# A planner that keeps TensorE's rows divided, and layer-0 aggregations noted one behind the other

## The chip, the cores and the metric

The kernel runs on one core of a Trainium2 chip. The metric is the device time of one execution in microseconds (us). The kernel before takes 3310.98 us, the median of three runs (3309.94 to 3311.04).

## What is computed

x holds 128 graphs of 64 nodes with 512 features each, all float32; adj is one 64 x 64 matrix of zeros and ones that all graphs share. Four layers follow one another, each as `x = layernorm(x + layer(x, adj))`:

```python
# layer 0: messages weighted by adj
out = deg * (x @ Wi.T + b) + adj @ (x @ Wj.T)
# layer 1: attention with 4 heads, attention with one, then two dense layers and a layernorm
h   = elu(softmax(mask(leaky(f1_i + f2_j))) @ (x @ W_heads))      # 4 heads, side by side
o   = elu(softmax(mask(leaky(g1_i + g2_j))) @ (h @ W_out))
y   = relu(o @ w1 + b1) @ w2 + b2 + o                             # then layernorm, gamma, beta
# layers 2 and 3: attention with one head
out = softmax(mask(leaky(e_src_i + e_dst_j))) @ (x @ W)
```

## The kernel before, in words

**Tiles.** Two graphs of 64 nodes fill the 128 partitions of one tile; two tiles make a pair (T = 2), and there are 32 pairs, p = 0 to 31. A pair goes through all four layers before it leaves the chip. Many pairs are under way at once, about one new one every 100 us.

**Products.** Most dense products are done in Strassen's way: `seven` (L633) makes seven products of halves where eight would be needed. It keeps two PSUM tiles, named stx and sty in the profile (sty holds two quarters of the result, y and z). Products 0, 2 and 4 go into sty, products 1, 3, 5 and 6 into stx, and each time VectorE (DVE) adds the result to its place in SBUF before the next product may start in the same tile. stx_h and sty_h are the heads of layer 1, stx_o and sty_o the projection by W_out, stx_y and sty_y the product by w2; stx_0, stx_2 and stx_3 are layers 0, 2 and 3 (the profile leaves the numbers out). The weights for these products are prepared once: `stage_stream` (L580) loads the four quarters of a matrix (raw_wo, raw_w, raw_W), lets GpSimd (POOL) form their differences T1 to T4, and stores all seven to a buffer in HBM (d_wo, d_w, d_W); `part_from` (L613) loads a part from there for each product (ws_wo, ws_w, ws_W). The raw quarters and the parts of the larger matrices share one ring of four SBUF buffers.

**Aggregations.** Where adj (or an attention matrix) is applied to x, a graph has only 64 nodes, so a matmul would use only 64 rows of TensorE. The kernel divides the rows: two matmuls, one per graph, stand in the upper and the lower 64 rows. This is so in `stage_first` (L887, layer 0: axp from x and aggr), in `stage_scores` (L937, layer 1's heads: yp from x and aT) and in `stage_out` and `stage_tile` (op from who and aT, 64 rows by 64 columns). Everything else uses all 128 rows. Layer 0's aggregation of one tile is eight matmuls into two PSUM tiles; ScalarE (ACT) copies them to the buffer ax, of which there is one. The first four pairs (p < AHEAD = 4) then multiply by W0 directly (l0); the later ones go through `strassen` with the stored parts of W0.

**Attention.** Scores come from dot products on DVE (or, for pairs 0 and 1, from a small matmul fp on transposed x, x1Tp); bc is their broadcast on TensorE, e the softmax on DVE and ACT, pt the transposed result, aT (aTg in layers 2 and 3) its copy by ACT, gp the aggregation in layers 2 and 3, oTp a transpose before w1, hidp the product by w1.

**What sets the order.** No instruction is issued where it is written. Every stage is a generator; the stages are run by a queue with due times (L1300 to L1330), and each call on an engine is only noted as a Step (`note`, L188). Calls inside `nc.together()` make one Step. A Step's rank is its place in the order of noting, less SOON = 1000 inside `nc.soon()`, plus corrections from the table LATER (L48), by engine and name and, with /S and /E, for the first 11% and the last 7% of the Steps only. Then `order` (L229) plays through all Steps with a simple cost of each (`cost`, L353): whenever an engine is free, it gets the ready Step of lowest rank. PSUM and SBUF buffers are handed out in this play as well: a Step that opens a tile waits for a free buffer, in the order of noting, and NEAR (L42) says how far a later Step may go ahead of an earlier one. SLACK (L43) is time allowed for a result to reach another engine. The order found is then issued, and each engine runs its own part in that order. SyncE (SP) issues all DMAs, so its order is that of the loads and stores.

Of the kernel before, what the change touches and what calls it, by code (L numbers as in the profile page):

```python
# [38 lines left out]


WAIT = 0.152
NEAR = 150  # L42
SLACK = {"tensor": 0.8, "sync": 0.4}  # L43

LATER = {  # L48
    "gp:never/S": -100, "gp:rs_i": -60, "gp:s_o/S": -20, "gp:ys/E": -40, "sc:aT": -100,
    "sc:aTg/S": 20, "sc:elu/S": -40, "sc:hT": 120, "sc:oT": 60, "sc:who": -80, "sc:xT": -200,  # L50
    "sc:xT/S": -180, "sc:ys/S": 132, "sy:beta/S": -12, "sy:raw_w": 180, "te:fp/S": -20,
    "te:hidp/E": -40, "te:hidp/S": 28, "te:l": 29, "te:l/S": 69, "te:pt": -28, "te:pt/E": 200,
    "ve:e": -29, "ve:e/S": 40, "ve:f_o/S": -120, "ve:hT": 100, "ve:has": 200, "ve:mv": -100,
    "ve:mv/E": 100, "ve:mx": -20, "ve:o": -140, "ve:r": -40, "ve:r/E": 40, "ve:sh": 10,
    "ve:sm": -80, "ve:st": -13,
}


# [105 lines left out]
class Plan:  # L164
# [23 lines left out]
    def note(self, engine, name, args, kw):  # L188
        if self.joined:
            s = self.joined[0]  # L190
            assert s.engine == engine
        else:
            s = Step(engine, len(self.steps) - self.early)
            self.steps.append(s)
            if self.joined is not None:
                self.joined.append(s)
        out = [kw[k] for k in ("out", "accum_out") if k in kw] + (
            [] if "out" in kw or not args else [args[0]]
        )
        views = [(v, True) for v in out if isinstance(v, View)] + [  # L200
            (v, False)
            for v in [*args, *kw.values()]
            if isinstance(v, View) and not any(v is o for o in out)
        ]
        for v, writes in views:
            t = v.tile
            writes = writes or t.pool.space is PSUM
            if not t.seen:
                s.opens.append(t)
            else:  # L210
                s.behind.add(t.seen[0][0])
            s.uses.add(t)
            s.after.update(o for o, r, w in t.seen if (w or writes) and v.meets(r))
            t.seen.append((s, v.region, writes))
        s.after.discard(s)
        s.behind -= {s} | s.after
        s.calls.append((name, args, kw))
        if not s.kind:
            what = out[0].tile.args.get("name", "?") if out and isinstance(out[0], View) else "dram"
            what = re.sub("__+", "_", re.sub(r"\d+", "", what).rstrip("_"))  # L220
            s.kind = f"{engine[:2]}:{what}"
        takes, s.lands = cost(engine, name, args, kw, out)
        if engine in ("vector", "gpsimd"):

            both = [v for v, writes in views if not writes and v.tile.pool.space is not PSUM]
            s.port = len(both) > 1 and (engine == "vector" or size_of(out) > 2)
        s.takes += takes

    def order(self):  # L229
# [2 lines left out]
        free = dict.fromkeys(engines, 0.0)  # L232
        coming = {e: [] for e in engines}
        there = {e: [] for e in engines}
        wire, port, out = 0.0, 0.0, []
        then = {s: [] for s in self.steps}
        for i, s in enumerate(self.steps):
            s.no, s.ready, s.waits = i, 0.0, len(s.after) + len(s.behind)
# [54 lines left out]
        while len(out) < len(self.steps):  # L293
            at, e = min(
                (free[e] if there[e] else max(free[e], coming[e][0][0]), e)
                for e in engines
                if there[e] or coming[e]
            )
            while coming[e] and coming[e][0][0] <= at:
                s = heapq.heappop(coming[e])[3]  # L300
                heapq.heappush(there[e], (s.rank, s.no, s))
            s = heapq.heappop(there[e])[2]
            if s.port and port > at:
                at = port
# [48 lines left out]
def cost(engine, name, args, kw, out):  # L353

    size = size_of(out)
    if engine == "tensor":
        if name == "transpose":
            return size * 0.00085, 0.0

        beside = P * P // math.prod(kw["lhsT"].shape)  # L360
        return (
            size * 0.00169 if beside == 1 else 0.208 / beside + 0.0003 * size
        ), 0.0
    if engine == "sync":
        return 0.06, 0.0015 * size
    if name == "tensor_tensor_reduce":
# [7 lines left out]
def gnn_stack_kernel(  # L374
# [512 lines left out]
    def stage_first(p):  # L887
# [3 lines left out]
            yield 0.3 * TURN  # L891

        ax = unit.tile([P, 2, T, KC, P], FP, tag="ax", name=f"ax_{p}")
        for t in range(T):
            x = xs[p][:, t, :]
            ps = [
                psum.tile([P, KC, 2, N], FP, tag="b", name=f"axp_{p}_{t}_{b}")
                for b in range(2)
            ]
            with nc.together():  # L900
                for c in range(KC):
                    for b in range(2):
                        nc.tensor.matmul(
                            ps[b][:, c, :, :], lhsT=x[ts(b, N), ts(c, P)],
                            rhs=aggr[ts(b, N), 0 if p < AHEAD else t, :, :], start=True, stop=True,
                        )
            with nc.soon():
                for b in range(2):
                    nc.scalar.copy(
                        ax[:, :, t, :, ts(b, N)], ps[b].rearrange("p c s i -> p s c i")  # L910
                    )
            nc.gpsimd.tensor_tensor(x, x, degb, ALU.add)
            yield 3.0
            if p < AHEAD:
                ps = psum.tile([P, D], FP, tag="b", name=f"l0_{p}_{t}")
                for k in range(KC):
                    with nc.together():
                        for s in range(2):
                            nc.tensor.matmul(
                                ps, lhsT=ax[:, s, t, k, :], rhs=w0[s][:, k, :],  # L920
                                start=(k == 0 and s == 0), stop=(k == KC - 1 and s == 1),
                            )
                    if k == 1:
                        yield 4.0
                nc.vector.tensor_tensor(x, ps, x, ALU.add)
                normalize(x, f"0_{p}_{t}")
                yield 4.0
        if p >= AHEAD:
# [464 lines left out]
```

## Time and profile before

| | |
|---|---|
| median of three runs | 3310.98 us |
| the profiled execution | 3313.95 us |
| its span, first to last instruction | 3312.2 us |
| mean granted TensorE clock | 0.994 |
| TensorE busy | 3265.2 us (99%), 21268 passes |
| VectorE (DVE) busy | 2374.4 us (72%) |
| GpSimd (POOL) busy | 1724.0 us (52%) |
| ScalarE (ACT) busy | 1364.6 us (41%) |
| DMA queue, share of 16 engines | 67.1%, 722 MB |

PE is TensorE's matmul, PEld its weight load. A line of the timeline gives the start, the length, the engine, the line of the code (nearly all have L336, as one helper issues everything), what is written from what, the rows and columns in use (64*128 is a divided matmul), and how many instructions are merged. A float32 matmul appears as two passes, a transpose as one. A line of waits gives the waiting engine and tile, whom it waited for, and the total, the number and the longest. A line of the table by stage gives the stretch, its width, the busy time of each engine with its number of instructions, the mean granted TensorE clock, the share of DMA and GB/s.

### The profile page before, as it was taken

To read this page: it belongs to the slowest core of one execution; us is meant where nothing else is said; L and a number is where in the kernel's file an instruction comes from. 1 tells how busy PE (TensorE), PEld (TensorE's weight loads), DVE (VectorE), ACT (ScalarE), POOL (GpSimd) and SP (SyncE) were. 2 spreads that over 40 slices of the span, in tenths; PEclk is the share of its full clock that TensorE was granted. 3 is DMA by queue.
4 is the path that set the end of the run, shared out by engine and by line. 5 is a ranking of instruction groups with operands and counts; after the bars stand their busy time and mean duration, and the time that the engine had idled before them with its cause. 6 is when DMAs were issued, how large, how long until landed. Compare 5 with 4: busy or idle time off the path is not lost.

```text
span 3312.2 us, 60000 instructions
## 1 busy us (share of the span) xinstructions
PE 3265.2 (99%) x21268; PEld 2881.8 (87%) x21268; DVE 2374.4 (72%) x5668; ACT 1364.6 (41%) x3226; POOL 1724.0 (52%) x1860
## 2 busy tenths in 40 slices
PE   8999999999999999999999999999999999999997
PEld 4888888898988989989889988888889899898885
DVE  5467767777777777777777777777777767777766
ACT  2434344343444434444443443434444344343442
POOL 6745445554555555455454555645554455554442
PEclk9999999999999999999999999999999999999998
DMA  8956666767667676667766667676666766667652
GB/s 303 338 177 215 221 203 215 234 208 237 211 210 233 213 247 197 200 230 221 242 204 220 212 217 236 214 226 208 214 233 208 246 201 202 229 216 238 227 183 77
DMA packets 306584, 726.08 MB, mean 219 GB/s; under 512 B 34240, under 2 KB 43504, under 8 KB 306288
## 3 DMA queue, kind: packets, MB, share of 16 engines
q1 hardware_dynamic: 306288, 722.26, 67.1%
q8 instruction: 171, 2.80, 0.3%
q14 instruction: 125, 1.02, 0.1%
HBM read 688.69 MB, written 33.44 MB: 218 GB/s over the span
## 4 chain that ended last, share of the span: by engine, by line
PE 91%; DVE 4%; DMA 3%; POOL 1%; issue 1%; ACT 0%; SPq 0%; POOLq 0%; DVEq 0%; ACTq 0%
PE stx_h L336 13%; PE stx_o L336 13%; PE stx L336 12%; PE sty_h L336 10%; PE sty_o L336 9%; PE sty L336 9%; PE hidp L336 7%; PE yp L336 4%; PE gp L336 3%; PE stx_y L336 3%; PE sty_y L336 2%; PE axp L336 2%; PE l L336 1%; PE op L336 1%; PE oTp L336 1%; DMA d_f<-f 1%
## 5 line engine op out<-in xcount | busy, mean ns | idle before, releaser
L336 DVE CUSTOM_DVE_ANT_0 j<-x,rows 128x512 bf16<-128x512 f32 x736 | 584.1, 794 | 94.3 <-DMA rows<-d_h 75.6
L336 PE MATMUL stx_h<-ys,wh 128*128 128x128 f32 x3072 | 403.8, 275 | 0.7 <-DVE hT L336 0.7
L336 PEld LDWEIGHTS stx_h<-ys,wh 128*128 128x128 f32 x3072 | 381.1, 192 | 22.3 <-DVE sh L336 5.7
L336 POOL TENSOR_SCALAR rs<-mv 128x1 f32<-128x1 f32 x256 | 104.1, 407 | 406.2 <-DVE mv L336 392.2
L336 ACT COPY hT<-stx_h 128x256 f32<-128x256 f32 x384 | 143.0, 372 | 384.6 <-PE stx_h L336 378.6
L336 ACT ACTIVATE x<-x,sh,rs 128x512 f32<-128x512 f32 x256 | 207.2, 813 | 223.6 <-DVE sh L336 221.0
L336 PE MATMUL sty_h<-ys,wh 128*128 128x128 f32 x2048 | 273.8, 277 | 0.0
L336 PEld LDWEIGHTS sty_h<-ys,wh 128*128 128x128 f32 x2048 | 254.4, 192 | 9.0 <-issue 0.5
L336 PE MATMUL stx_o<-ws_wo_T,s_o 128*128 128x256 f32 x1024 | 246.0, 383 | 0.5 <-ACT who L336 0.5
L336 DVE TENSOR_TENSOR x<-stx,x 128x256 f32<-128x256 f32 x360 | 150.8, 420 | 132.1 <-PE stx L336 131.0
L336 PE MATMUL sty_o<-ws_wo,hT 128*128 128x256 f32 x1024 | 243.2, 380 | 0.1
L336 PE MATMUL hidp<-oT,w 128*128 128x256 f32 (+1 forms) x1056 | 228.9, 373 | 0.0
L336 PEld LDWEIGHTS hidp<-oT,w 128*128 128x128 f32 x1056 | 194.0, 190 | 24.9 <-ACT oT L336 0.2
L336 PEld LDWEIGHTS stx_o<-ws_wo_T,s_o 128*128 128x128 f32 x1024 | 190.2, 191 | 28.4 <-ACT who L336 2.1
L336 PEld LDWEIGHTS sty_o<-ws_wo,hT 128*128 128x128 f32 x1024 | 190.8, 191 | 25.6 <-issue 1.1
L336 DVE SCALAR_TENSOR_TENSOR hT<-elu,hT 128x512 f32<-128x512 f32 x256 | 174.9, 684 | 43.3 <-ACT elu L336 41.3
L336 POOL TENSOR_TENSOR ys<-ys,t 128x256 f32<-128x256 f32 x128 | 102.9, 814 | 189.8 <-PE sty_h L336 189.4
L336 ACT ACTIVATE elu<-hT 128x512 f32<-128x512 f32 x256 | 153.0, 599 | 108.7 <-DVE hT L336 104.6
L336 POOL TENSOR_TENSOR rs<-rs,mhalf 128x1 f32<-128x1 f32 x256 | 173.4, 677 | 21.1
L336 DVE BATCH_NORM_STATS2 st<-x 128x6 f32<-128x512 f32 x256 | 176.5, 689 | 5.1
L336 DVE TENSOR_TENSOR hT<-sty_h,hT 128x256 f32<-128x256 f32 x256 | 107.2, 420 | 81.2 <-PE sty_h L336 69.3
L336 ACT COPY ys<-yp 128x512 f32<-128x512 f32 x256 | 132.2, 602 | 78.4 <-PE yp L336 71.7
(205 smaller groups left out, 7629.3 us busy)
## 6 DMA issues: line engine op xcount, KB each, us to landing
ws_wo_T<-d_wo_T SPq DMA_DIRECT2D x256, 512.0 KB, 3.9
ws_wo<-d_wo SPq DMA_DIRECT2D x192, 512.0 KB, 5.3
ws_W_T<-d_W_T SPq DMA_DIRECT2D x248, 256.0 KB, 4.2
rows<-d_h SPq DMA_DIRECT2D x240, 256.0 KB, 4.7
ws_w_T<-d_w_T SPq DMA_DIRECT2D x112, 512.0 KB, 4.9
ws_W<-d_W SPq DMA_DIRECT2D x186, 256.0 KB, 4.1
ws_w<-d_w SPq DMA_DIRECT2D x84, 512.0 KB, 5.2
rows<-d SPq DMA_DIRECT2D x128, 256.0 KB, 4.3
```

Of the source, the lines that this page charges most:

```text
L336: getattr(getattr(self.tc.nc, s.engine), name)(*map(real, args), **{k: real(v) for k, v in kw.items()})
```

## The change

Four things change together:

1. `note` marks a matmul whose stationary operand is smaller than 128 x 128 as tiled. When the planner chooses TensorE's next Step and the last one was tiled, it takes a ready tiled Step ahead of all others.
2. The planner's costs: a change between tiled and other Steps takes 0.2 us; a tiled matmul is priced by half its columns.
3. In `stage_first`, for pairs from 4 on, the aggregations of both tiles are noted directly one behind the other, ahead of ACT's copies; before, tile 1's came after tile 0's copies and an addition on POOL. For the first four pairs the order of noting is as before.
4. NEAR goes from 150 to 176, SLACK for sync from 0.4 to 0.403, and the table LATER has other entries, so that ranks move on every engine.

```diff
-NEAR = 150
-SLACK = {"tensor": 0.8, "sync": 0.4}
+NEAR = 176
+SLACK = {"tensor": 0.8, "sync": 0.403}
...
-    "gp:never/S": -100, "gp:rs_i": -60, "gp:s_o/S": -20, "gp:ys/E": -40, "sc:aT": -100,
...
+    "gp:ax": -120, "gp:raw_w/S": 60, "gp:raw_wo/S": -60, "gp:rs_i": -40, "gp:rs_i/E": -60,
+    "gp:t": -160, "gp:t/E": 100, "gp:ys": 20, "sc:elu": -112, "sc:f/S": -80, "sc:who/S": -120,
+    "sc:x": 40, "sc:ys": -160, "sc:ys/S": 120, "sy:b_sb/S": -80, "sy:beta/S": -3,
+    "sy:d_w_T": -260, "sy:d_wo_T": 100, "sy:degb": -120, "sy:w": 40, "sy:wh": 7, "te:bc_o": -80,
+    "te:fp": -60, "te:gp/E": 11, "te:hidp/S": 28, "te:l/S": 131, "te:pt/E": 200,
+    "te:stx/S": -20, "te:stx_h/E": 27, "te:stx_y/S": -28, "te:sty_o/E": -240, "te:xTp": -120,
...
+        s.tiled = "lhsT" in kw and math.prod(kw["lhsT"].shape) < P * P
...
-            s = heapq.heappop(there[e])[2]
+            s = None
+            if rows and e == "tensor":
+
+                more = [c for c in there[e] if c[2].tiled]
+                if more:
+                    s = min(more)
+                    there[e].remove(s)
+                    heapq.heapify(there[e])
+                    s = s[2]
+            s = s or heapq.heappop(there[e])[2]
+            if e == "tensor":
+                at += 0.2 * (s.tiled != rows)
+                rows = s.tiled
...
-        return (
-            size * 0.00169 if beside == 1 else 0.208 / beside + 0.0003 * size
-        ), 0.0
+        return size * 0.00169 / beside + 0.005 * (beside > 1), 0.0
...
         ax = unit.tile([P, 2, T, KC, P], FP, tag="ax", name=f"ax_{p}")
+        ps = {}
+
+        def turn(t):
+            for b in range(2):
+                ps[t, b] = psum.tile([P, KC, 2, N], FP, tag="b", name=f"axp_{p}_{t}_{b}")
+            for c in range(KC):
+                for b in range(2):
+                    nc.tensor.matmul(
+                        ps[t, b][:, c, :, :], lhsT=xs[p][ts(b, N), t, ts(c, P)],
+                        rhs=aggr[ts(b, N), 0 if p < AHEAD else t, :, :], start=True, stop=True,
+                    )
+
+        if p >= AHEAD:
+            for t in range(T):
+                with nc.together():
+                    turn(t)
         for t in range(T):
             x = xs[p][:, t, :]
-            ps = [
-                psum.tile([P, KC, 2, N], FP, tag="b", name=f"axp_{p}_{t}_{b}")
-                for b in range(2)
-            ]
-            with nc.together():
-                for c in range(KC):
-                    for b in range(2):
-                        nc.tensor.matmul(
-                            ps[b][:, c, :, :], lhsT=x[ts(b, N), ts(c, P)],
-                            rhs=aggr[ts(b, N), 0 if p < AHEAD else t, :, :], start=True, stop=True,
-                        )
+            if p < AHEAD:
+                with nc.together():
+                    turn(t)
```

More of the change, by code (lines that the diff above doesn't have):

```diff
@@ L41 @@
 WAIT = 0.152
-NEAR = 150
-SLACK = {"tensor": 0.8, "sync": 0.4}
+NEAR = 176
+SLACK = {"tensor": 0.8, "sync": 0.403}
 LATER = {
-    "gp:never/S": -100, "gp:rs_i": -60, "gp:s_o/S": -20, "gp:ys/E": -40, "sc:aT": -100,
[L50 to L55, printed above, removed]
+    "gp:ax": -120, "gp:raw_w/S": 60, "gp:raw_wo/S": -60, "gp:rs_i": -40, "gp:rs_i/E": -60,
[4 more added lines that the diff above has]
+    "te:stx/S": -20, "te:stx_h/E": 27, "te:stx_y/S": -28, "te:sty_o/E": -240, "te:xTp": -120,
+    "ve:abd": -120, "ve:e": -29, "ve:e/S": 40, "ve:e_o/E": 140, "ve:f_o/E": 160,
+    "ve:f_o/S": -120, "ve:gT": 340, "ve:mv": -100, "ve:mv/E": 140, "ve:mv_i/E": -80,
+    "ve:o": -100, "ve:r": -60, "ve:sh": 49, "ve:sm": -60, "ve:st": -20, "ve:st_i": -20,
+    "ve:st_i/S": -40, "ve:who": -140,
 }
@@ L234, in order @@
         there = {e: [] for e in engines}
-        wire, port, out = 0.0, 0.0, []
+        wire, port, rows, out = 0.0, 0.0, False, []
         then = {s: [] for s in self.steps}
@@ L909, in stage_first @@
                     nc.scalar.copy(
-                        ax[:, :, t, :, ts(b, N)], ps[b].rearrange("p c s i -> p s c i")
+                        ax[:, :, t, :, ts(b, N)], ps[t, b].rearrange("p c s i -> p s c i")
                     )
@@ L914, in stage_first @@
             if p < AHEAD:
-                ps = psum.tile([P, D], FP, tag="b", name=f"l0_{p}_{t}")
+                l0 = psum.tile([P, D], FP, tag="b", name=f"l0_{p}_{t}")
                 for k in range(KC):
@@ L919, in stage_first @@
                             nc.tensor.matmul(
-                                ps, lhsT=ax[:, s, t, k, :], rhs=w0[s][:, k, :],
+                                l0, lhsT=ax[:, s, t, k, :], rhs=w0[s][:, k, :],
                                 start=(k == 0 and s == 0), stop=(k == KC - 1 and s == 1),
@@ L924, in stage_first @@
                         yield 4.0
-                nc.vector.tensor_tensor(x, ps, x, ALU.add)
+                nc.vector.tensor_tensor(x, l0, x, ALU.add)
                 normalize(x, f"0_{p}_{t}")
```

## The prediction, made before the changed kernel ran

> **What bounds the kernel now.** First the busy times, for the whole span and by stage; then TensorE's waits; then its timeline at the places that these name; last, the instruction orders of both kernels. Page, part 1:
>
> ```profile
> span 3312.2 us, 60000 instructions
> PE 3265.2 (99%) x21268; PEld 2881.8 (87%) x21268; DVE 2374.4 (72%) x5668; ACT 1364.6 (41%) x3226; POOL 1724.0 (52%) x1860
> ```
>
> TensorE is the bound. By stage (width, then busy time by engine):
>
> ```profile
> 0.00:300.00 300.00, 281.89 (x1710) 224.09 (x1711) 179.12 (x423) 112.61 (x257) 178.86 (x169) 0.98 0.76 259
> 300.00:3200.00 2900.00, 2894.01 (x19159) 2591.96 (x19158) 2123.51 (x5044) 1216.36 (x2874) 1512.11 (x1635) 1.00 0.68 220
> 3200.00:3313.00 113.00, 89.27 (x403) 65.73 (x401) 71.75 (x203) 35.62 (x96) 33.08 (x57) 0.89 0.29 92
> ```
>
> In the loop TensorE is idle 6 of 2900 us; the head and the tail have 18 and 24. So a gain can come only from fewer TensorE microseconds of work, or from head and tail. A matmul here is two passes. A pass's price is start to start over its count (TensorE's timeline: start, length, group):
>
> ```profile
> 1502.92 1.03 PE L336 MATMUL sty<-ws_W_T,gT 128*128 128x256 f32 x4
> 1503.78 1.05 PE L336 MATMUL stx_h<-ys,wh 128*128 128x128 f32 x8
> 1504.67 1.03 PE L336 MATMUL stx<-ws_W_T,s 128*128 128x256 f32 x4
> ```
>
> ```profile
> 1029.12 1.89 PE L336 MATMUL stx_o<-ws_wo_T,hT 128*128 128x256 f32 x8
> 1030.95 2.95 PE L336 MATMUL yp<-aT,x 64*128 64x128 f32 x48
> 1033.83 1.99 PE L336 MATMUL stx<-ws_w_T,s 128*128 128x256 f32 x8
> 1035.75 0.49 PE L336 MATMUL yp<-aT,x 64*128 64x128 f32 x4
> ```
>
> Four 256-column passes take 0.86 us (0.215 each), eight 128-column passes 0.89 (0.111). Divided passes go two at a time: 24 pairs should take 24 x 0.111 = 2.67 us. Now the switches: before the divided stretch 8 x 0.215 = 1.72, but 1.83 are used (+0.11); the stretch uses 2.88 (+0.21); the eight passes after it 1.92 (+0.20, of which about half belongs to the next stretch). **One stretch of divided rows costs 0.40 us** for going in and out, whatever its length. Priced so, TensorE's starts leave 28 us lost at 0 to 300, 11 in the loop, 28 after 3200 (half-speed passes counted too). TensorE's waits in the head (total, times, longest), then in the tail:
>
> ```profile
> PE stx_o L336 <- DVE who L336: 2.5, 1, 2.5
> PE x1Tp L336 <- ACT ax L336: 2.0, 1, 2.0
> PE pt_1o L336 <- DVE e_1o L336: 1.6, 1, 1.6
> PE sty_h L336 <- POOL t L336: 1.5, 1, 1.5
> PE stx_o L336 <- DMA ws_wo<-d_wo: 1.1, 1, 1.1
> ```
>
> ```profile
> PE bc L336 <- DVE f L336: 6.0, 3, 3.5
> PE sty L336 <- ACT gT L336: 2.4, 1, 2.4
> ```
>
> **What the Trainium skill says.** "TensorEngine Tiling (Array Packing)", Key Properties: a change of tiling mode drains TensorE. The trace agrees: 0.40 us per stretch. "TensorE: Matmul & The Clock Gate", Part 1: the clock has two rates, full and half, decided in windows of about 3.4 us. The trace agrees: the 2 us wait of x1Tp at 66 us is followed by layer-0 passes of 0.85 us in place of 0.43, and the window 70 to 74 us has a mean clock of 0.72. So a wait of 2 us can cost a further 1 to 2. "DMA: Bandwidth & Descriptors", Queues, rings and completion order: each DMA engine takes descriptors in ring order. At the start the landings do follow SP's order, about 0.65 us per 256 KB.
>
> **Part 1, the switches.** Both orders hold the same matmuls (10,996 calls), so only stretches count. Before: 165 (71 of yp, 62 of axp, 32 of op). After: 158 (65, 55, 32, and 6 of axp with yp). The rule does little: the two axp groups of a pair stand next to each other in one of the 28 later pairs; in the others a PSUM buffer comes free 2.1 to 5.1 us of TensorE work later, and something else goes in between. 7 x 0.40 = **-2.8 us**, all on the bound. Lower price 0.2 (only the drain in): -1.4; higher 0.5: -3.5.
>
> **Part 2, the start.** The new table reorders SP's queue: degb (256 KB) and b1 go ahead of adj; x_1, x_2, x_3 ahead of w0; rows_a and wh between w0's chunks. adj landed at 2.7 and 3.4 us and TensorE began at 4.7; behind degb I put it 2 us later (nearest row: degb took 1.7 us in its place; range 1 to 4). In return pair 1's aggregation, which had to await x_1 until 15.3 us, now fills early time, while w0's last chunk (some 6.5 MB down the queue, which the trace of before had moved by 21.5 us) comes at about 22 us and is wanted at about 25. To the first axp of pair 2 I count 28.2 us after, 28.4 before: **0**, range -1 to +4. DVE now has six wh dot products ahead of the first x_0 addition; their weights land by about 21.6, the addition is due at 26: no cost.
>
> **Part 3, x1Tp.** It stood behind ax's copies, which wait for the one ax buffer, which waits for l0_2_1. Its wait and the slow passes after it cost 2.15 + 0.39 + 1.35 = 3.9. In the new order x1Tp of pair 1 goes 13 us of work earlier; what now follows l0_2_1 is bc (0.86), half of fp (0.9), then l0_3_0, which needs two ax copies (2 x 0.59 and some 0.5 on the way, 1.7): covered, up to 0.3 left. **-3.8**, range -3.9 to -2.
>
> **Part 4, the first projection.** At 126 to 134 us TensorE loses 1.67 + 0.35 + 1.23 = 3.3 to POOL's t1 and the load of ws_wo. POOL does t1 two long operations earlier in the new order, so the first wait goes (-3.3). But TensorE then comes some 5 us earlier to a chain that does not move with it: the four ws buffers pass from raw_wo1 to raw_w0 to ws_wo, released by POOL's raw_w0 operations (2.36 us each) and by stores and loads of 4 to 5 us. Raw_w0's third operation ends at about 122 us in place of 124.4, as t1 and t2 (2 x 1.27) now stand ahead of it; the first ws_wo lands 5 us later, at 127; TensorE is there at 122.5. New wait **+4.2**, range 0 to +7. Behind it on TensorE's queue everything waits.
>
> **Part 5, 195 to 290 us.** The last product of pair 1's projection waited for DVE's addition to who with 0.4 us of work in between; now 2.2. With yp behind it, 2.70 + 0.57 + 1.13 = 4.4 were lost; I leave 0.9: **-3.5**, range -4.4 to -1. gp of pair 0 after pt: 0.53 + 1.05 lost, cover 1.1 and 2.6 us in place of 0.9 and 0.9: **-1.3**. oTp of pair 0 has lost one 1.7 us group of its cover: **+0.5**, range 0 to 1.5. The wait at pt_1o of pair 0 (2.7 of work between bc_1o and pt_1o in both) stays.
>
> **Loop and tail: 0.** Loop links keep their cover: pt to gp 2.6 us or more in both, op to oTp 4.7 and 4.8, pt to yp 3.6 in place of 1.9. Thinner are axp to the first product of layer 0 (3.2 us in six pairs, never under 5.8; it needs about 1.7) and pt_1o to op (2.9 for 3.6). The tail has the same sequence from hidp of pair 31 on, and two of its largest waits stand at the same places (bc of pair 30, gT of pair 30). Range -2 to +4 for both together.
>
> **Sum.** -2.8 + 0 - 3.8 - 3.3 + 4.2 - 3.5 - 1.3 + 0.5 = **-10.0**. The profiled execution took 3313.95 (span 3312.2 and 1.8 around it), so 3304.0 in its terms; the median of the runs is 3.0 below it, 3310.98, so **3301.0**.
>
> **Rivals.** (a) The head's waits only move: POOL, stores and loads are as late as before, and parts 3 to 5 give nothing. For it: POOL is busy 179 of the first 300 us, and part 4 is such a case. Against it: x1Tp and who had their causes in the order alone. Left: part 1, 3308.2. (b) The chain of part 4 moves along with TensorE (POOL's earlier operations start earlier, as they hang on DVE's dot products): no new wait, -14.2, 3296.8. (c) Slower: two aggregations noted behind one another hold four of the eight PSUM buffers until ACT has copied them, and the first product of layer 0 follows in six of the 28 pairs after 3.2 us. If that starves TensorE by more than 10.0/28 = 0.36 us in each of 28 pairs, the gain is gone; at 0.85 (24 us in all) it ends at 3325. Against it: in the loop ACT waits for axp (215 us in all) and TensorE never waits for ax there. (d) The change doesn't do what it says: taken into part 1, as 165 to 158 shows.
>
> **Chances.** The forecast 0.43; (b) 0.19; (a), with a late start or half of parts 3 and 5 missing, 0.28; (c) 0.10. A difference of 0.2% (6.6 us) is about what a measurement here can tell from no change: faster means under 3304.4, slower over 3317.6. The forecast and (b) are faster, 0.62; (a) is the same, 0.28; (c) slower, 0.10. Range: from part 1 to 5's better ends, 3293, to (a) with the start 3 us late, 3311; outside lie (c) and a little at either end.
>
> **What would show it.** Part 1: divided stretches 158 in TensorE's timeline, each still 0.40. Part 2: TensorE's first matmul at 6 to 7 us, pair 2's axp at 28. Part 3: no wait of x1Tp. Part 4: a wait of sty_o or stx_o for ws_wo of about 4 us near 122 to 128. Part 5: who's wait under 1 us. Loop: idle time as before, under 10 us. I am wrong if the loop shows a wait that repeats with every pair, or if the head's loss stays near 28 us.

## The result: slower by 6 us, and the profile after

| | before | after |
|---|---|---|
| median, 18 runs each | 3310.28 us | 3316.74 us |
| ratio, 95% interval | | 1.0017 (1.0011 to 1.0024) |
| span of the profiled execution | 3312.2 us | 3317.1 us |

The forecast was 3301.0, its range 3293 to 3311: wrong in sign. Page of the changed kernel, part 1:

```profile
span 3317.1 us, 59898 instructions
PE 3263.4 (98%) x21268; PEld 2880.5 (87%) x21268; DVE 2363.1 (71%) x5668; ACT 1364.7 (41%) x3226; POOL 1697.4 (51%) x1860
```

TensorE's passes are as many as before. By stage (width, then busy time by engine, the last three columns the mean TensorE clock, the DMA engines' busy share and GB/s):

```profile
0.00:300.00 300.00, 281.65 (x1720) 225.82 (x1721) 184.50 (x425) 113.87 (x258) 176.45 (x170) 0.98 0.77 261
300.00:3200.00 2900.00, 2887.63 (x19117) 2586.18 (x19116) 2103.52 (x5028) 1213.97 (x2871) 1483.84 (x1630) 1.00 0.68 219
```

In the loop TensorE is idle 12.4 us where it was idle 6.0. The prediction's own measure, the time between TensorE's starts beyond the prices of passes and switches ("the loss" from here on), sorts the 4.9 us between the two spans (the last column is a second profile of the changed kernel):

| loss, us | before | after | after again |
|---|---|---|---|
| ahead of the first matmul | 4.7 | 5.2 | 5.8 |
| 0 to 100 | 11.0 | 8.2 | 7.6 |
| 100 to 200 | 11.0 | 17.1 | 13.2 |
| 200 to 300 | 6.5 | 0.5 | 0.8 |
| loop, 300 to 3200 | 11.1 | 22.3 | 23.1 |
| tail | 27.4 | 26.1 | 26.8 |

The switches give back their 2.8 us, the stretch from the first matmul to 300 us 2.7 (in the second profile 6.9) and the tail 1.3; the first matmul comes 0.5 later, and the loop takes 11.2. TensorE's waits in the loop, before and then after (total, times, longest):

```profile
PE pt L336 <- DVE e L336: 1.9, 2, 1.1
PE sty_y L336 <- DMA ws_w<-d_w: 1.3, 2, 0.9
PE stx_o L336 <- DMA ws_wo_T<-d_wo_T: 1.1, 2, 0.6
```

```profile
PE sty_y L352 <- DMA ws_w<-d_w: 3.2, 7, 0.8
PE stx_o L352 <- DMA ws_wo_T<-d_wo_T: 2.5, 6, 0.9
PE pt L352 <- DVE e L352: 1.6, 2, 1.0
PE sty_y L352 <- DMA ws_w_T<-d_w_T: 1.2, 2, 0.7
```

In the changed kernel no wait is longer than 1 us, but there are many, and the new ones are above all for DMAs, for the parts of w2 that sty_y and stx_y multiply by. Counted as loss, the products of w2 went from 2.9 us to 10.9. These parts come through the second ring of the kernel (six buffers of 256 KB for the parts of w2, W2 and W3): a load can leave only when a buffer comes free, a median of 6.5 us ahead of its use and in a quarter of the cases under 5.2, and then has to land. In the kernel before it is the same: 6.6, and a quarter under 5.2. So the change did not take time from these loads. The page's DMA view (count, size, median us from issue to landing) of before, then of after:

```profile
ws_w_T<-d_w_T SPq DMA_DIRECT2D x124, 256.0 KB, 3.6
ws_w<-d_w SPq DMA_DIRECT2D x93, 256.0 KB, 2.9
```

```profile
ws_w_T<-d_w_T SPq DMA_DIRECT2D x124, 256.0 KB, 4.2
ws_w<-d_w SPq DMA_DIRECT2D x93, 256.0 KB, 3.9
```

These medians rest on 37 and 45 of w2's 217 loads, those whose landing the page tells. Worked out from the semaphore updates in the trace for 215 of the 217, the mean went from 4.1 to 4.5 us and the median from 4.0 to 4.3; the slowest quarter begins at 5.2 us in place of 4.6. So the same transfers take some 0.4 us longer in the new order, and most of it lies in the slow ones.

### The profile page after: what moved, and what is told of

It reads as the page before. It is cut to its first block, busy times and chain, and to the rows that moved or that the text cites. A ratio compares the mean times of both kernels' runs of the same rounds, so it can differ in the third digit from the quotient of the medians.

```text
span 3317.1 us, 59898 instructions
## 1 busy us (share of the span) xinstructions
PE 3263.4 (98%) x21268; PEld 2880.5 (87%) x21268; DVE 2363.1 (71%) x5668; ACT 1364.7 (41%) x3226; POOL 1697.4 (51%) x1860
## 4 chain that ended last, share of the span: by engine, by line
PE 88%; DMA 6%; DVE 3%; POOL 2%; issue 1%; SPq 0%; ACT 0%; POOLq 0%; DVEq 0%; ACTq 0%
PE stx_h L352 13%; PE stx_o L352 12%; PE stx L352 11%; PE sty_h L352 10%; PE sty_o L352 9%; PE sty L352 8%; PE hidp L352 7%; PE yp L352 3%; PE gp L352 3%; PE stx_y L352 2%; PE l L352 2%; DMA over<-d_f 2%; PE axp L352 1%; PE sty_y L352 1%; DMA ws_wo_T<-d_wo_T 1%; DMA d_f<-f 1%
## 5 line engine op out<-in xcount | busy, mean ns | idle before, releaser
L352 POOL TENSOR_SCALAR rs<-mv 128x1 f32<-128x1 f32 x256 | 88.7, 347 | 387.8 <-DVE mv L352 334.5
L352 POOL TENSOR_TENSOR s<-gT 128x256 f32<-128x256 f32 x62 | 48.1, 776 | 225.3 <-DVE gT L352 169.0
L352 DVE SCALAR_TENSOR_TENSOR sh<-mv,rs 128x1 f32<-128x1 f32 x256 | 105.3, 412 | 79.9 <-POOL rs L352 79.5
```

What stands on the lines that cost most here:

```text
L352: getattr(getattr(self.tc.nc, s.engine), name)(*map(real, args), **{k: real(v) for k, v in kw.items()})
```

## The experiments

Labels with a_ are edits of the changed kernel, with b_ of the kernel before. Each ran beside the kernel before on the same chip; "ratio" is to it. The kernel before took between 3308.0 and 3312.3 us beside them, so experiments are compared by their ratios, not by their times. With half-widths of about 0.0008, two ratios are told apart from some 0.001 (3.5 us) on.

**Is it the ring, the start, or what is in the way?** a_wk7 and b_wk7: `bufs` of the ring 6 to 7 in the real tiles only, so no order changes. To make room, layer 0's bias rows are added where beta's belong, which leaves beta out of the result (that edit isn't shown).

```diff
+MORE = {'wk': 7}
...
-            self.made = self.pool.real.tile(self.shape, self.dtype, **self.args)
+            args = dict(self.args)
+            if args["tag"] in MORE:
+                args["bufs"] = MORE[args["tag"]]
+            self.made = self.pool.real.tile(self.shape, self.dtype, **args)
```

> The changed kernel, every engine's order as it is, but with 7 buffers in place of 6 in the ring that holds the parts of w2, W2 and W3 (to make room, POOL adds layer 0's bias rows where beta's rows belong; beta is still loaded, into a tile that nothing reads). My theory: of the 11.2 us that the loop lost against the kernel before, 8.0 stand ahead of products of w2, whose parts are loaded only when a buffer of this ring comes free, 4 to 7 us before their use, and land 4 to 5 us later. A seventh buffer lets each load start one part earlier (about 0.9 us or more), so the losses at w2's products fall from 10.9 us to 1 to 3 us and the kernel is 7 to 10 us faster than the changed one: 3307 to 3310, ratio to the kernel before 0.999 to 1.000. Rival, late starts elsewhere: the losses at w2's products only mark where TensorE meets a delay of DVE or POOL that stands behind it; then they move to another product and the time stays within 2 us of 3316.7. Rival, two aggregations holding four of eight PSUM buffers: no effect, 3316 to 3317.

> The kernel before with the same seventh buffer and the same substitution of bias rows. My theory: its products of w2 lose only 2.9 us in the loop, so it gains 1 to 3 us: 3307 to 3309, ratio 0.9990 to 0.9997, and the two kernels then stand within 2 us of each other where they stood 6.4 apart. Rival, delays of other engines: no gain here either, and the difference of 6 us stays.

a_wk7: 3313.27 us, 1.0007 (0.9999 to 1.0015): against the changed kernel's 1.0017 and 1.0022 a gain of 3 to 5 us, at the edge of what can be told apart and about half of what I had expected. Loads left 0.6 to 0.7 us earlier, but w2's mean landing time rose from 4.5 to 4.9 us; the loss at w2's products fell only to 9.2. b_wk7: 3311.03, 1.0000 (0.9992 to 1.0009), no gain; there too the landing time rose, from 4.1 to 4.4. In both, about half of the head start was lost again on the way.

a_start puts three loads back in front, a_rows moves two broadcasts behind a part of w2, both on SP's queue alone (a_start's edit is shown):

```diff
-            for s in self.order():
+            out = self.order()
+            first = [s for s in out if s.kind in ("sy:adj_i", "sy:x")][:3]
+            for s in first + [s for s in out if s not in first]:
```

> The changed kernel with one edit: on SP's queue the two loads of adj and the first of x_0 go ahead of degb and b1 again, all else as in the changed kernel. The prediction put the late start at 0 up to pair 2's first aggregation. My theory now: TensorE's first matmul comes 1 to 2 us earlier and part of that reaches the first projection at 96 us, where TensorE then waits for ws_wo all the same; so it gains 0 to 2 us, 3315 to 3317. Rival: the start is the larger part of the missing gain in the head, and the kernel is 3 us or more faster.

> The changed kernel with one edit: in the 13 pairs whose score rows of layer 2 (two broadcasts of 256 KB) are issued between w2's parts 21 and 22, SP issues them behind part 22; every other engine's order is the same. My theory: what makes w2's loads late is the company that they land in; without these two transfers ahead of them T2 and 22 land about 1 us or more earlier in these 13 pairs, whose losses at w2's products (3.4 us in sum) go, and the kernel is 2 to 4 us faster, 3313 to 3315. Rival, the ring alone sets the landing (loads start as late as before): less than 1 us.

a_start: 3317.81, 1.0020 (1.0014 to 1.0027), nothing gained: the first matmul came at 4.1 us but the first aggregation at 8.0 (7.0), and pair 2's at 28.5 (27.9). a_rows: 3319.44, 1.0028 (1.0017 to 1.0039), nothing gained either. In its profile w2's products lost 7.5 us in place of 10.9, as expected, but the loop still lost 23.1: pt lost 5.1 (2.8), sty_o 5.0 (1.7). The loss had moved.

**Which part of the change?** v1_oldtable keeps rule and costs and takes the old table, NEAR and SLACK; v4_norule takes the rule out (`s = heapq.heappop(there[e])[2]`, no 0.2); v6_lat3 plans landings 1 us later (`s.end = wire + 3.0`).

> The changed kernel (rule for divided rows, price of a switch and of divided matmuls, both tiles' aggregations noted together) with the table, NEAR and SLACK of the kernel before. The order that it gives has 149 divided stretches (158 in the changed kernel, 165 before), 16 x 0.40 = 6.4 us less of switches than before. My theory: it is the new table that sets w2's loads among other transfers, not the rule; then the loop loses 11 to 15 us (22.3 in the changed kernel), of which 3 to 5 at w2's products, and the kernel runs in 3304 to 3310. Rival, the rule: taking divided groups out of their rank makes every just-in-time load tighter; then the loop loses 18 us or more here too, and the time is 3312 or more.

> The changed kernel with its new table, costs and noting, but without the rule in the planner: TensorE's next group is again the first by rank, and no switch is priced. 160 divided stretches, 0.8 us more of switches than the changed kernel. My theory (the table): the loop loses 18 us or more, 3314 to 3320. Rival (the rule): the loop loses about 11 us as before the change, and with the head's gains of 2.7 us the time is 3305 to 3310.

> The changed kernel with one number changed in the planner: a load is planned to land 3.0 us after its transfer in place of 2.0 (parts of w2 take 4.5 us from issue to landing in the trace of the changed kernel, 2.8 in the old plan). 147 divided stretches, 4.4 us less of switches. My theory: the loop's losses are loads that land later than planned, so with 1 us more planned the losses at w2's products fall from 10.9 to 2 to 5 us, and the kernel runs in 3303 to 3309, faster than the changed one by 8 to 13 us. Rival: TensorE then meets the next tight thing (the attention chain before pt, POOL's sums before the projection's products), as in the run with the score rows moved; then the loop loses 17 us or more and the gain is that of the switches alone, 3310 to 3313.

> The changed kernel once more, as a reference beside the others, and for a second profile of it: how far do the losses of one execution repeat? My theory: the loop loses 20 to 26 us again, 9 to 13 of it at w2's products, and the time is 3315 to 3318. Rival: the losses at w2's products are those of one execution; then they fall under 5 us here.

v1_oldtable 3370.34 (1.0180, 1.0166 to 1.0194), v4_norule 3345.49 (1.0108, 1.0093 to 1.0123), v6_lat3 3370.55 (1.0180, 1.0166 to 1.0194), after_again 3318.13 (1.0022, 1.0013 to 1.0030). The first three loop losses are 68, 36 and 68 us, spread over almost every product.

All three expectations were too low by 25 to 60 us; of the rivals only v1_oldtable's, which was open upward (3312 or more), holds the result. Rule and table can't be judged apart: in these runs each half without its own other half costs far more than the 6 us in question, so splitting them says nothing of either. One part can be split off: with the rule, costs and table of the changed kernel, noting both tiles' aggregations behind one another (point 3 of the change) makes no difference at all. The planner's order is the same on all five engines without it. The second profile confirms the loop's loss (23.1, of which 13.1 at w2's products).

**Taking TensorE's waits away, all transfers made, orders unchanged.** a_free and b_free let w2's products read resident columns; a_wo does so for pair 0's first projection. (The condition on `dims` leaves the loads themselves as they are.)

```diff
+                if v.tile.args.get("name", "").startswith("ws_w2") and v.dims != [0, 1, 2]:
+                    v = self.w1[:, v.region[1][0], 0:256]
+                return v.real()
```

> The changed kernel with every load and every engine's order as they are, but the products of w2 read columns of w1, which are resident, in place of the parts of w2 that are loaded for them; so TensorE no longer waits for these loads (the second matrix of the feed-forward layer is left out of the result; the transfers are all still made). Known by now: the loop of the changed kernel loses 22.3 and 23.1 us in two profiles, 10.9 and 13.1 of it at w2's products; moving other transfers out of the way of w2's loads lowered that to 7.5 but pt and the projection's products lost 6 us more. My theory: the late loads of w2 are the loss that the change added; without them the loop loses 11 to 14 us and the kernel runs 8 to 12 us faster than the changed one, 3305 to 3309, ratio to the kernel before 0.998 to 0.9995. Rival: the order is tight everywhere, and TensorE, being earlier, meets the attention chain and POOL's sums instead; then the loop loses 18 us or more and at most 4 us are gained, 3312 or more.

> The kernel before with the same edit: w2's products read resident columns of w1, all loads and orders stay. Theory: its loop loses 2 to 3 us at w2's products, so it gains 1 to 4 us, 3307 to 3310, and stands within 2 us of the changed kernel with the same edit, or behind it. Rival: no gain, 3310 to 3313, and the changed kernel with the edit stays 3 us or more behind it.

> The changed kernel, all loads and orders as they are, but the seven products of pair 0's first projection read columns of w1 in place of the loaded parts of W_out (that piece of the projection is left out of the result for this pair). It prices the new wait of part 4: in two profiles TensorE waited 4.2 and 4.1 us at its first product for the load, and passes at half speed and a second wait followed, 9 to 10 us less 2 in sum. Theory: the loss from 100 to 200 us falls from 13 to 17 us to 5 to 8, and the kernel is 6 to 9 us faster, 3308 to 3311. Rival: POOL's sums or the who additions stand right behind the load, and 3 us or less are gained.

a_free: 3318.63, 1.0024 (1.0015 to 1.0033). b_free: 3312.31, 1.0002 (0.9994 to 1.0011). My theory fell: TensorE no longer waited for w2, and nothing was gained. Loop and waits of a_free:

```profile
300.00:3200.00 2900.00, 2886.20 (x19111) 2586.41 (x19110) 2103.46 (x5030) 1213.57 (x2870) 1482.27 (x1630) 1.00 0.68 219
```

```profile
PE pt L357 <- DVE e L357: 5.9, 6, 1.3
PE sty L357 <- DMA ws_w<-d_w: 2.6, 4, 1.1
PE stx L357 <- DVE x L357: 1.6, 3, 0.6
```

TensorE is as idle as in the changed kernel (13.8 us; 12.4 there), and the loop loses 22.0 us: pt 7.3 where it was 2.8.

The edit had a side effect, though. Where no product reads a buffer, the next load into it waits for the landing of the one before, and SP's queue is held at other places. SP's own waits in the loop, in the changed kernel and in a_free:

```profile
SPq L352 <- DMA ws_w<-d_w: 1.1, 3, 0.5
SPq L352 <- DMA ws_w_T<-d_w_T: 2.5, 6, 0.7
```

```profile
SPq L357 <- DMA ws_w<-d_w: 50.5, 38, 3.8
SPq L357 <- DMA ws_w_T<-d_w_T: 12.2, 19, 1.7
```

In return, SP's waits for stx_y and sty_y fell from 84 us to 10. So part of what a_free lost elsewhere may be of its own making, and that it gained nothing doesn't prove that w2's waits cost nothing.

a_wo: 3318.29, 1.0022 (1.0014 to 1.0030), no gain; the wait for ws_wo, 4.0 us at the first group of the projection, came as 5.7 us at the next group of the same projection, and 100 to 200 us lost 14.3 (17.1 and 13.2 in the changed kernel).

**A second chain beside the first.** The pt that wait over 1 us in a_free are those of pairs 8, 16, 18, 24 and 26, in the heads' attention. Its way is f2p (TensorE), a store d_f, two loads over, DVE's e, pt. In pairs 8, 10, 16, 18, 24 and 26 the change cut TensorE's work between f2p and pt from 26.8 us to 23.4. The first part of the way has grown as well. Pair 16 before (TensorE's, SP's and DVE's timelines):

```profile
1606.25 0.27 PE L336 MATMUL f2p<-ident,f 128*8 128x128 f32 x1
...
1633.15 0.60 PE L336 MATMUL pt<-ident,e 128*128 128x128 f32 x4
```

```profile
1605.85 0.92 SPq L336 DMA_DIRECT2D ws_w_T<-d_w_T  x2
1606.86 0.29 SPq L336 DMA_DIRECT2D d_f<-f  x1
...
1611.76 1.12 SPq L336 DMA_DIRECT2D over<-d_f  x2
```

```profile
1630.90 0.69 DVE L336 TENSOR_TENSOR e<-bc,r 128x512 f32<-128x512 f32 x1
```

and after:

```profile
1607.62 0.27 PE L352 MATMUL f2p<-ident,f 128*8 128x128 f32 x1
...
1631.37 0.63 PE L352 MATMUL pt<-ident,e 128*128 128x128 f32 x4
```

```profile
1608.79 1.18 SPq L352 DMA_DIRECT2D ws_w_T<-d_w_T  x2
1610.07 0.29 SPq L352 DMA_DIRECT2D d_f<-f  x1
...
1615.27 1.10 SPq L352 DMA_DIRECT2D over<-d_f  x2
```

```profile
1630.53 0.69 DVE L352 TENSOR_TENSOR e<-bc,r 128x512 f32<-128x512 f32 x1
```

Before, d_f leaves 0.6 us after f2p's start; after, 2.4, since it stands on SP's queue behind parts T3 and T4 of w2, which wait for their buffers; over leaves 7.6 us after f2p in place of 5.5. e is done at 1631.22, pt starts 0.15 later, so it was waited for; before, e was done 1.56 us ahead of pt. (From f2p to e's end it is 23.6 us; before it was 25.3, with nothing that hurried it.) So two chains run beside each other, w2's loads and this one. In the changed kernel itself this one costs little: pt of the six pairs lost 1.9 us in all, 1.0 in the second profile. In a_free it lost 6.1, and there d_f left 3.1 us after f2p in the mean of the six, in place of 2.5, so the side effect above has its part in it. a_df and a_fix move DMAs on SP's queue, a_free_df joins a_free and a_df:

```diff
+            for p in range(6, 31):
+                df, q = at[f"d_f_1_{p}"], p - 2
+                behind = [f"ws_w2_{q}_T3", f"ws_w2_{q}_T4"]
...
+                        if at[b] < df:
+                            spot[at[b]] = df + 0.1 + 0.1 * k
...
+                        spot[w] = over + 0.4
```

Here b is one of the two parts in `behind`, w the load of W2's part 11; a_fix also puts rows_2 of pair q, where they stand amid w2's parts, behind T4.

> The changed kernel with SP's order edited in six pairs (8, 10, 16, 18, 24, 26) and nothing else: the store d_f, on which pair p's head attention hangs, goes ahead of parts T3 and T4 of w2 (for pair p-2), and part 11 of W2 goes behind the loads of over. Known by now: in these six pairs the work that TensorE has between f2p and pt fell from 26.8 us to 23.4 by the change, while the way from f2p by d_f, over and DVE's softmax to pt takes 24.5, because d_f stands on SP's queue behind T3 and T4, which wait for buffers until 1.9 us after f2p (0.5 us in the kernel before). My theory: TensorE's late loads of w2 and this chain run beside each other, and the later of the two decides; so this edit alone takes away the waits at pt (2.8 us, 1.2 a pair at most) and leaves those at w2's products: 0 to 3 us faster than the changed kernel, 3314 to 3317. Rival: the chain alone paces the loop, and the edit gives 5 us or more.

> Both at once: w2's products read resident columns of w1 (the second matrix of the feed-forward layer is left out of the result; all transfers are made), and d_f goes ahead of T3 and T4 as in the run with that edit alone. My theory: taking away the waits for w2 alone gave nothing because pt then waited 1.17 us in these six pairs (7.3 us in all at pt). With both gone the loop loses 13 to 16 us in place of 22, and the kernel runs 5 to 9 us faster than the changed one, 3308 to 3312. Rival: a third thing stands close behind (the projection's products behind POOL, layer 0's behind ax); then the loop still loses 19 us or more and the time stays at 3314 or more.

> A version that computes everything: the changed kernel with SP's order edited as for d_f alone and, in the 13 pairs where the score rows of layer 2 stand amid w2's loads, these rows behind part T4. The run that moved the rows alone lowered the losses at w2's products from 10.9 to 7.5 us, but put the rows ahead of d_f, and pt lost 2.4 us more. My theory: with d_f ahead of both, pt loses under 2 us, w2's products about 7, the loop 14 to 18, and the kernel is 3 to 7 us faster than the changed one: 3310 to 3314, about as fast as the kernel before. Rival: SP's order in these places is not what costs; less than 2 us.

a_df 3316.84 (1.0024, 1.0014 to 1.0033), a_free_df 3315.94 (1.0024, 1.0014 to 1.0033), a_fix 3321.56 (1.0038, 1.0025 to 1.0050). With w2's waits gone and d_f moved, a_free_df's loop still lost 24.0 us, now at layer 0's product sty (4.6, most of it waits for the loads of its weights), stx_y (4.7), pt (3.9), sty_o (3.4). In a_fix d_f landed in 2.0 to 2.8 us in place of 4.4 to 5.5, and over in 7.0 to 8.0 in place of 4.7 to 6.0: what one transfer gained another lost. (a_df's profiled execution lost only 16.7 us in the loop, at a span of 3310.6; its ratio is that of the changed kernel, so one execution doesn't show a gain.)

**Taking transfers away.** That pattern suggests a resource shared by all these waits. From 4 to 8 us after f2p of pair 16, before and then after (last columns: clock, DMA share, GB/s):

```profile
1610.36:1614.36 4.00, 4.00 (x34) 3.38 (x33) 1.81 (x3) 2.19 (x5) 0.98 (x2) 1.00 0.99 348
```

```profile
1611.73:1615.73 4.00, 4.00 (x23) 3.36 (x21) 2.27 (x6) 0.00 (x0) 0.00 (x0) 1.00 1.00 358
```

The DMA engines are full there in both orders, though they are busy only 0.68 over the loop. The Trainium skill, "DMA: Bandwidth & Descriptors", section "Issuing engines are not separate DMA queues", says that all DMAs run on the same 16 DMA engines and interleave, whichever engine starts them. Here SP starts them all, so no run tests other starters; that DMAs share what there is, a_fix's d_f and over show with the numbers above. a_now2 and b_now2 leave w2's loads out (1.8 MB of about 22 MB a pair), a_norows and b_norows the score rows of layer 2 (0.5 MB).

```diff
+                if s.engine == "sync" and kw_name(s).startswith("ws_w2"):
+                    continue
                 for name, args, kw in s.calls:
```

> The changed kernel without the loads of w2's parts (31 pairs, seven of 256 KB each): its products read resident columns of w1, so the second matrix of the feed-forward layer is left out of the result; every other instruction stays in its place. Unlike the run that kept these loads, this one takes the transfers away: around f2p the 16 DMA engines were busy 0.85 to 1.01 in the even pairs of the changed kernel. My theory: in these stretches it is the sum of the transfers that sets when the last of them lands; whatever stands first, another waits, which is why no single wait could be taken away with profit. Without 1.8 MB a pair d_f, over and the rest land 1 us or more earlier, the loop loses 8 to 14 us in place of 22, and the kernel is 7 to 13 us faster than the changed one: ratio to the kernel before 0.998 to 1.000. Rival: DVE's and POOL's parts of the chains pace the loop; then the loop still loses 18 us or more and the ratio stays at 1.001 or more.

> The kernel before without the loads of w2's parts, products reading w1 as in the other run. The transfers' theory: its loop loses only 11 us with them, so little is gained, 0 to 5 us, ratio 0.9985 to 1.000, and the changed kernel without these loads comes level with it or ahead of it by the 2.8 us of switches and 2.7 us of the head. Rival: the changed kernel stays 4 us or more behind it.

> The changed kernel without the loads of the score rows of layer 2 (two broadcasts of 256 KB a pair): DVE's dot products read resident rows of w1 in their place, so layer 2's scores are wrong ones; all else stays. The rows stand amid w2's loads in 13 pairs. The transfers' theory: 0.5 MB less in the busy stretches take 3 to 6 us off the loop's 22, and the kernel is 2 to 6 us faster than the changed one, ratio 1.0000 to 1.0012. Rival: no gain, ratio 1.0015 or more.

> The kernel before without the loads of the score rows of layer 2 (DVE's dot products read resident rows of w1, so layer 2's scores are wrong ones). The changed kernel without them was 1.0001 of the kernel before, some 6 us faster than with them. My theory: the busy stretches of the order before leave room for these 0.5 MB a pair (they stand amid w2's loads in 10 pairs of 29, and a part of w2 follows closer behind them in few), so they cost it little: 0 to 3 us, ratio 0.9990 to 1.0000. Rival: they cost any order the same 5 to 7 us, ratio 0.9985 or less, and then they explain nothing of the difference.

| | after: time | ratio | loop's loss | before: time | ratio | loop's loss |
|---|---|---|---|---|---|---|
| as it is | 3316.74 | 1.0017 (1.0011 to 1.0024) | 22.3 | 3310.28 | 1 | 11.1 |
| w2's waits gone | 3318.63 | 1.0024 (1.0015 to 1.0033) | 22.0 | 3312.31 | 1.0002 (0.9994 to 1.0011) | 10.6 |
| w2's transfers gone | 3302.35 | 0.9982 (0.9975 to 0.9989) | 8.7 | 3302.94 | 0.9986 (0.9980 to 0.9993) | 7.5 |
| rows' transfers gone | 3307.06 | 1.0001 (0.9993 to 1.0009) | 14.4 | 3311.96 | 1.0000 (0.9992 to 1.0008) | 8.9 |

(w2's waits gone: a_free and b_free; w2's transfers: a_now2 and b_now2; the rows': a_norows and b_norows, which ran on different chips.) The loop of a_now2 and of a_norows:

```profile
300.00:3200.00 2900.00, 2895.46 (x19178) 2600.81 (x19177) 2108.74 (x5052) 1219.79 (x2883) 1492.11 (x1635) 1.00 0.62 202
```

```profile
300.00:3200.00 2900.00, 2894.04 (x19151) 2594.53 (x19150) 2104.89 (x5042) 1217.98 (x2876) 1487.08 (x1634) 1.00 0.66 214
```

Without w2's transfers TensorE is idle 4.5 of 2900 us in the changed kernel (3.6 in b_now2), and the two kernels are level; the changed one has won about 12 us by it, the one before 5. The rows' 0.5 MB cost the changed kernel about 5.5 us (1.0017 to 1.0001) and the kernel before nothing that can be told (its interval is 2.6 us to either side). In a_norows w2's parts land sooner:

```profile
ws_w_T<-d_w_T SPq DMA_DIRECT2D x124, 256.0 KB, 3.4
ws_w<-d_w SPq DMA_DIRECT2D x93, 256.0 KB, 3.1
```

Again these medians rest on few loads (22). Over 210 of the 217 the mean is 3.8 us, where it was 4.5 with the rows and 4.1 in the kernel before; the loads leave as long ahead of their use as with the rows (7.0 us in the mean, 7.1); and w2's products lose 6.5 us less than in the changed kernel.

So the loop's added loss hangs on transfers: the changed kernel's loop loses 11.2 us more than the other's with all of them, 5.5 more without the rows', 1.2 more without w2's (one profile each), and in both cases without them the two ratios are level. For w2's loads it is the time on the way that matters, since they leave no earlier in a_norows. For the attention chain I can't say it so simply. To leave a transfer out does two things: it frees the DMA engines, and it frees SP's queue, where a load that waits for its buffer holds back all that stands behind it. In the six pairs of a_now2 d_f lands 1.2 to 1.5 us after its issue (4.4 to 5.5 in the changed kernel), but it also leaves 1.5 us after f2p in place of 2.5. So a_free and a_now2 differ in more than the transfers, and how much of the loss is DMA time and how much is SP's queue is not shown.

Nor is it shown why the new order suffers more than the old one. Three features of it fit: rows of layer 2 amid w2's parts in 13 pairs of 29 (10 before), d_f behind w2's parts, and 3.4 us less of TensorE's work over the attention chain in six pairs. No edit of SP's order alone mended it, and no version that computes everything beat the kernel before.

## Why the prediction was wrong, point by point

- **Sum.** From the start to 300 us (parts 2 to 5) I had forecast -7.2; the table above has -2.2, and -5.8 in the second profile. The loop, forecast at 0, took +11.2 and +12.0.
- **Part 1, right.** 158 stretches, and priced at 0.40 they leave the losses above: -2.8.
- **Part 2, right in what it comes to.** Pair 2's first axp came at 27.9 us (28.2 after again; forecast 28.2, before 28.4). The late start was smaller than I had put it: the first matmul came at 5.2 us (5.8 after again) and not at 6 to 7, the first aggregation at 7.0, 1.0 later than before. a_start shows that the place of degb and b1 is worth nothing that can be told.
- **Part 3, right.** No wait of x1Tp is left, and 0 to 100 us lost 2.8 us less (3.4 in the second profile; forecast 3.8).
- **Part 4, right in kind, too small.** The new wait was 4.0 us (forecast 4.2). The wait for POOL's t at 126 to 128 us is gone, but one of 1.2 us for another t stands at 92.6. Two waits of the changed kernel from 0 to 300 us, and TensorE's timeline at the first:

```profile
PE sty_o L352 <- DMA ws_wo<-d_wo: 4.0, 1, 4.0
PE stx_o L352 <- DMA ws_wo_T<-d_wo_T: 2.1, 1, 2.1
```

```profile
124.75 1.06 PE L352 MATMUL stx_h<-ys,wh 128*128 128x128 f32 x8
129.82 2.74 PE L352 MATMUL sty_o<-ws_wo,hT 128*128 128x256 f32 x8 [4.01 <-DMA ws_wo<-d_wo]
132.63 2.55 PE L352 MATMUL stx_o<-ws_wo,hT 128*128 128x256 f32 x7
```

  Eight passes of 0.215 should take 1.7 us and took 2.7, start to start 2.8: a part of them ran at half speed after the wait. The Trainium skill, "TensorE: Matmul & The Clock Gate", Part 1, has the half clock follow an idle window of about 3.4 us. The trace agrees, with a mean granted clock of 0.50 from 130.9 to 134.3 us; but it was 0.50 again from 141.1 to 144.5, after the second wait of only 2.1 us, so here less than a whole window sufficed. I had named that price for x1Tp and left it out here. With it and the second wait (stx_o for the next part) the place lost 10.1 us in place of 4.2; the second profile has 3.9 us of waiting, half-speed passes after it and no second wait. (TensorE stopped at 125.6, not at 122.5.) a_wo shows that this wait has the rest of the same stream of loads right behind it.
- **Part 5, right in kind.** 200 to 300 us lost 0.5 us where it had lost 6.5: -6.0 against the -4.3 of its three terms, a little beyond their better ends (-5.7).
- **Loop and tail: 0. This step failed.** The tail is right (-1.3 and -0.6). The loop took +11.2 where I allowed +4. I looked at links whose cover I could count in TensorE's work (pt to gp, op to oTp, pt to yp) and saw two others get thinner, none too thin; two kinds I did not look at. One is the link from f2p to pt, which goes by two DMAs and lost 3.4 us of 26.8 in six pairs; in the changed kernel's profiles it cost 1.0 to 1.9 us. The other is the ring of w2's parts, and it is the larger: +8.0 of the +11.2 stand at w2's products. Their loads have a median of 6.5 us between release and use, in both orders; their landing time I took as given, while it went from 4.1 to 4.5 us in the mean and fell to 3.8 when the rows around them were left out. An order without times shows the first link and not the second.
- **Rival (c)** ended on the right side for a wrong reason: axp lost 1.3 us in the loop, 1.0 before, so PSUM held by two aggregations starves nothing, and noting them together does not even move an instruction. (a) holds for part 4 alone. (d) is true of that noting, which part 1 had half seen.
- The sign that I had named, a wait that repeats with every pair, was not there in that form. w2's products lost over 0.3 us in 13 of the loop's 29 pairs (4 before), and in the second profile in 15, in part others, though the order is the same.

## What to carry to other kernels

When TensorE is 99% busy and many waits of under 1 us come up in new places, don't take them away one by one: look for what they share. Here a DMA share of 0.68 on average hid stretches at 1.00, and leaving transfers out showed what leaving waits out had not. Look also at what else such an edit moves: loads whose buffers nobody read held the DMA queue at other places, and loads that were left out freed the queue as well as the engines. A median over few of the transfers can mislead, too; count how many it rests on. Before trusting a new order, count for each chain that crosses DMAs the work that covers it, and list what else is issued into the same few microseconds; a planner's table fits only the rule and the costs with which it was made (36 to 68 us lost in the loop otherwise).

## What the runs showed of the hardware that I had not expected

With a seventh buffer loads left 0.6 to 0.7 us earlier and took 0.3 to 0.4 us longer, so about half of the head start was lost on the way. The shortest of w2's 256 KB loads took 2.6 us from issue to landing, the mean one 4.1 in one order and 4.5 in the other, the longest 7.2 (8.3 in the second profile). A store of 4 KB (d_f in the six pairs) took 1.2 to 1.5 us without w2's transfers around it and 4.4 to 5.5 with them. TensorE's wait of 4 us for ws_wo was followed by 6 passes of 256 columns at about twice their price (0.43 for 0.215 us) in the first profile and by 13 in the second, 1.7 and 2.7 us on top of it.
